# Small products, sums and a relu placed anew in a four-layer convolution kernel

## The chip, the core and the metric

The kernel runs on one core of one Trainium2 chip. A core has five engines that take instructions side by side: TensorE (PE in the profile; PEld is its loading of weights), VectorE (DVE), ScalarE (ACT), GpSimd (POOL) and SyncE (SP), which here issues transfers. Transfers (DMA) are issued by SP and by POOL. The metric is the device time of one launch in microseconds (us); lower is better.

## What is computed

The input x is 4 images of 256 channels with 56 x 56 positions, float32. Four layers follow one another, each of the form x = x + layer(gn(x)), where gn is a group normalization over 32 groups of 8 channels. Cut to what matters here:

```python
def _gn(v, G=32, eps=1e-5):
    g = v.reshape(B_, G, C_ // G, H_, W_)
    m = jnp.mean(g, axis=(2, 3, 4), keepdims=True)
    s = jnp.var(g, axis=(2, 3, 4), keepdims=True)
    return ((g - m) / jnp.sqrt(s + eps)).reshape(v.shape)
...
# layer 0: an involution. 7x7 kernels computed from h = 256 -> 64 channels at each
# position, one kernel for each group of 16 channels
out = (kern * patches).sum(axis=3)
# layer 1: relu(y + bn(conv3x3(relu(bn(conv3x3(y)))))) with y = gn(x)
# layer 2: an involution with batch norm and relu on h, and on its output
# layer 3: a spectral gate, x * (sigmoid factor of the channel) + x * (factor of the position)
```

The statistics of each normalization need the whole image of the layer before, so the layers meet at their norms: sums over an image, an average over the 8 channels of a group, a reciprocal root, and a scale ("rstd") and a shift for each channel.

## The kernel before

**Involution layers (0 and 2), `involution_layer`.** The work goes in 8 units (image b, half cb of the channels). A unit has two stages. In the *tap stage* (`tap_matrices`, L602) 32 pairs of PSUM banks are filled by products L613 of hp (the reduced channels) with the span weights z_sb, and read out into kt, two of three by DVE (L634), one of three by ACT (L627). In the *column stage* seven columns of 8 positions each are done by `apply` (L646): the products L659 of the windows xw with kt come in two parts, each into a pair of banks of its own; ACT (L672 in layer 0, L674 in layer 2) and DVE (L679, three in part 1 and one in part 2) read them into un, and POOL (L684, layer 0) or DVE (L686, layer 2) adds un to x in place. After each `apply` the next windows are made: seven transposes L427 on PE into a pair of banks, a copy by ACT (L439) and four transfers by SP (L445, L446); then `next_strip` writes the next normalized strip (POOL L412; in layer 2 from the third on, ACT L410). Layer 2 first clears the strip (L391, POOL), and DVE clears its borders (L404, L406).

PSUM is handed out by `two_banks` and `one_bank` from one pool of four pairs that are taken in turn; whoever takes a pair waits for the last reader of what it held.

**The order of the work.** Each engine executes its instructions in program order. Work of other kinds is put between the stages by hand: `tap_matrices` takes a dictionary `hooks` of steps to be issued at the tap position n (n - 0.5 before its read-out), and the columns have lists `early[tx]` and `late[tx]`, issued before and after column tx. Generators are cut into such steps by their yields. `by_counts(g, counts)` (L247) joins several yields of g to one step, as many as each count says.

**Norms, `norm_steps` (L217).** It yields after each of: the aggregation of sums (L215, DVE), a product with the group averages (L226, PE), the copy of its result (L229), a difference (L233), its square (L235), the sum with the variance (L237, all DVE), a second product (L240, PE), the reciprocal root (`rsqrt_eps`: L150 on DVE, L151 on POOL), and the shift (L244, DVE). It is given a function that says in which bank the two products go. In the involution layers, `norm_of` (L988) gives it `spare[0]`: in the column stages this is the second bank of the pair that the last part of `apply` took (set at L652), in the tap stages the end of the bank in use. The norms of layer 0's next image are made in the column stages of the image before: for cb = 0 in columns 3 to 6 (`norm_first`), for cb = 1 in columns 1 to 3 (`norm_last`), followed there by the channel reduction of that image. The last image's first unit has the steps for layer 1's norm of the images before, and layer 2's first unit those of its own last image.

**Channel reduction, `bottleneck` (L451).** Four products L467 of the shift with the reduction weights, their result with bias and scale as hb (L478 in layer 2, DVE), then the products L489 of x, whose results ACT writes as hp (L508 in layer 2, 20 of them an image) and DVE copies to the other half (L497).

**The convolutions (layer 1), `conv_layer`.** They run in 12 chunks of rows, three an image (16, 20 and 20 rows). In `conv2` the product L1606 or L1591 of each of six filter positions is combined by DVE (L1618 to L1634 and L1807 to L1813), partly after a copy by ACT (L1617). `joined(co)` ends a chunk for half co of the channels. For all chunks but the last two the residual comes in by accumulating transfers (`leaves`), and the chunk's sums are made by ACT with `mean_of` (L1768) and `spread_of` (L1774), each of which writes over x and so follows the store of it. Chunk 10: DVE adds y (L1752), ACT makes the relu (L1764), POOL issues a transfer that adds the layer's input (L1765), SP stores (L1766), and the sums are made by DVE's bn_stats (L1784) at the start of chunk 11, in pieces of up to 8 rows. Chunk 11, the last: DVE adds y (L1752), DVE makes the relu and adds the input in one instruction (L1757), SP stores (L1758); its six bn_stats stand in layer 2, all at hook 3 of the first tap stage. `tail` is the list of steps that a chunk leaves for later.

The boundary of layer 1 and layer 2 is then: the last chunk on PE and DVE, the norm of image 0 (whose parts are ready before, L244 excepted), L467, hb, L489, L508, two strips and two sets of windows, and the first L613.

## Time and profile before

| | us |
|---|---|
| three runs | 1665.92, 1666.82, 1667.41 |
| their median | 1666.82 |
| profiled execution | 1665.74 |
| its span, first to last instruction | 1663.7 |
| around the span | 2.0 |
| PE busy | 1586.3 |
| DVE busy | 1328.1 |
| ACT busy | 1010.6 |
| POOL busy | 552.1 |
| a column of layer 0 without a norm product | 4.13 |
| a tap stage | 22.5 |

The mean clock granted to PE was 0.979 of the full one. How to read the lines that follow: a timeline line has the start and the busy time in us, the engine, the line of the kernel, the operation, output<-inputs by the program's names, the shape, how many instructions were merged, and in brackets how long the engine had been idle before and which engine, tile and line ended that idle time. A line of the waits has the engine and the line that waited, what it waited for, the total in us, how many times, and the longest. The page's line of engines gives busy us, the share of the span and the number of instructions; the line below it in the prediction gives the shares of the chain that ended last.

### The profile page before, as it was taken

Reading aid. Unit: us, or ns where it says so; the run is one execution under the profiler, and the core shown is the slowest. Engines: PE = TensorE matmul, PEld = TensorE weight load, DVE = VectorE, ACT = ScalarE, POOL = GpSimd, SP = SyncE. Lnnn points to the kernel's source line nnn. Section 1 sums busy time; section 2 is a strip of 40 time slices with the busy share of each in tenths; the row PEclk is TensorE's granted clock in tenths of the full one; section 3 lists DMA queues with packets and bytes.
Section 4 is the critical chain, followed back from the end, with each engine's and each line's share of the span. In section 5 each row is a group of like instructions: output and inputs, shape, how many; then the busy total and the mean of one; then the engine's idle time right before and its main releaser. Section 6 shows DMA issues by size and latency. Waiting matters only on the chain.

```text
span 1663.7 us, 57362 instructions
## 1 busy us (share of the span) xinstructions
PE 1586.3 (95%) x24600; PEld 1442.0 (87%) x24600; DVE 1328.1 (80%) x2391; ACT 1010.6 (61%) x2203; POOL 552.1 (33%) x764
## 2 busy tenths in 40 slices
PE   6999999999989999999999999988999899899998
PEld 4997998898888898899999999976888888788886
DVE  2686887787659988899999999987777678678775
ACT  1655655557446565666666567426677577577565
POOL 2133223322522343423333333200000662662671
PEclk9999999999999999999999999998999999999997
DMA  2363445444558977987788797744445765764753
GB/s 92 111 197 115 157 155 169 146 156 132 181 171 266 171 130 150 198 174 157 159 166 170 163 197 151 172 144 145 131 140 166 216 220 188 210 216 159 206 168 113
DMA packets 102875, 275.67 MB, mean 166 GB/s; under 512 B 15877, under 2 KB 43790, under 8 KB 98910
## 3 DMA queue, kind: packets, MB, share of 16 engines
q0 software_dynamic: 43856, 106.25, 31.3%
q1 hardware_dynamic: 57726, 164.48, 30.7%
q8 instruction: 195, 3.19, 0.8%
q10 hardware_dynamic: 1040, 1.26, 0.3%
q14 instruction: 58, 0.48, 0.1%
HBM read 95.07 MB, written 49.15 MB: 87 GB/s over the span
## 4 chain that ended last, share of the span: by engine, by line
PE 68%; DVE 13%; DMA 6%; issue 6%; ACT 4%; SPq 1%; POOL 1%; ACTq 0%; POOLq 0%; DVEq 0%
PE ps L613 21%; PE mm L1606 17%; PE ps L659 15%; PE mm L1591 6%; DVE un L679 3%; PE ps L427 3%; DMA xw<-xw 2%; DVE kt L634 2%; PE ps L489 2%; DMA xs<-x 1%; ACT hp L508 1%; DMA xs<-v 1%; SPq L445 1%; DVE st L380 1%; ACT xs L1737 1%
## 5 line engine op out<-in xcount | busy, mean ns | idle before, releaser
L659 PE MATMUL ps<-kt,xw 126*32 126x48 f32 (+1 forms) x12544 | 378.9, 235 | 23.1 <-DMA xw<-xw 9.6
L659 PEld LDWEIGHTS ps<-kt,xw 126*32 126x32 f32 (+1 forms) x12544 | 340.9, 121 | 66.3 <-issue 40.4
L613 PE MATMUL ps<-hp,z_sb 64*126 64x133 f32 x6144 | 376.0, 278 | 1.8 <-ACT hp L508 0.9
L613 PEld LDWEIGHTS ps<-hp,z_sb 64*126 64x126 f32 x6144 | 364.1, 186 | 13.1 <-DVE kt L634 6.0
L634 DVE TENSOR_TENSOR kt<-ps,zb_sb 126x798 f32<-126x798 f32 x352 | 331.9, 980 | 48.9 <-PE ps L613 29.8
L627 ACT ACTIVATE kt<-ps,zb_sb 126x133 f32<-126x133 f32 x960 | 280.5, 441 | 78.1 <-PE ps L613 78.1
L1606 PE MATMUL mm<-xs,u_sb 128*128 128x140 f32 (+2 forms) x1664 | 210.3, 279 | 4.2 <-DMA xs<-v 4.1
L1606 PEld LDWEIGHTS mm<-xs,u_sb 128*128 128x128 f32 x1664 | 200.8, 192 | 4.6 <-issue 4.5
L1591 PE MATMUL mm<-v,u_sb 128*128 128x280 f32 (+2 forms) x864 | 193.9, 383 | 2.4 <-DVE hp L1622 1.7
L1591 PEld LDWEIGHTS mm<-v,u_sb 128*128 128x128 f32 x864 | 161.6, 189 | 28.0 <-PE mm L1606 2.2
L684 POOL TENSOR_TENSOR xs<-un,xs 128x240 f32<-128x240 f32 x112 | 72.0, 663 | 298.8 <-DVE un L679 298.7
L679 DVE SCALAR_TENSOR_TENSOR un<-ps,s,un 128x240 f32<-128x240 f32 x224 | 102.5, 458 | 85.2 <-ACT un L674 79.2
L679 DVE SCALAR_TENSOR_TENSOR un<-ps,par_sb,un 128x240 f32<-128x240 f32 x224 | 97.7, 456 | 84.3 <-ACT un L672 80.2
L1574 POOL DMA_DIRECT2D xs<-v x100 | 96.6, 1003 | 182.8 <-ACT xs L1573 161.7
L672 ACT ACTIVATE un<-ps,par_sb 128x240 f32<-128x240 f32 x112 | 50.2, 448 | 131.8 <-PE ps L659 121.0
L439 ACT COPY xw<-ps 126x896 f32<-126x896 f32 x112 | 101.3, 905 | 39.8 <-PE ps L427 22.0
L427 PE MATMUL ps<-ident_sb,strip_sb 128*126 128x128 f32 x784 | 112.7, 285 | 5.2 <-POOL strip_sb L412 2.0
L674 ACT ACTIVATE un<-ps,bn_t,s 128x240 f32<-128x240 f32 x112 | 60.1, 538 | 92.3 <-PE ps L659 85.2
L427 PEld LDWEIGHTS ps<-ident_sb,strip_sb 128*126 128x126 f32 x784 | 85.8, 142 | 16.1 <-POOL strip_sb L412 3.7
L1606 PE MATMUL mm<-v_sb,u_sb 128*128 128x140 f32 (+2 forms) x688 | 95.2, 281 | 3.2 <-ACT u_sb L1353 1.8
L1606 PEld LDWEIGHTS mm<-v_sb,u_sb 128*128 128x128 f32 x688 | 88.4, 193 | 4.3 <-ACT u_sb L1353 2.0
L1573 ACT ACTIVATE xs<-v 128x560 f32<-128x560 f32 (+2 forms) x100 | 61.8, 629 | 44.3 <-DVE v L1518 35.9
(325 smaller groups left out, 2344.2 us busy)
## 6 DMA issues: line engine op xcount, KB each, us to landing
xw<-xw SPq DMA_DIRECT2D x224, 252.0 KB
xw<-xw SPq DMA_DIRECT2D x224, 126.0 KB
xs<-x POOLq DMA_DIRECT2D x24, 560.0 KB, 6.9
x<-xs POOLq DMA_DIRECT2D x8, 1568.0 KB, 8.1
xs<-x SPq DMA_DIRECT2D x8, 1568.0 KB
xs<-v POOLq DMA_DIRECT2D x44, 280.0 KB, 4.3
xs<-v POOLq DMA_DIRECT2D x42, 252.0 KB, 4.2
xs<-in_x_dram SPq DMA_DIRECT2D x6, 1568.0 KB
```

What stands on the lines that cost most here:

```text
L427: nc.tensor.transpose(ps[:Q, k * P : (k + 1) * P], flat[:, k * Q : (k + 1) * Q], ident_sb)
L439: nc.scalar.copy(xw[:, :NSB, :], ps[:Q, : NSB * P].rearrange("q (n c) -> q n c", n=NSB))
L613: nc.tensor.matmul(ps[:Q, i, k * NT : (k + 1) * NT], z_sb[i * R : (i + 1) * R, cb * GB // 2 + gp, z0 : z0 + Q], hp[i * R : (i + 1) * R, py ...
L627: nc.scalar.activation(kt[:, g0 + i, pb, :, k], ps[:Q, i, k * NT : (k + 1) * NT], AF.Identity, bias=zb_sb[:, cb * GB + g0 + i, p0 + k : p0 ...
L634: nc.vector.tensor_tensor(kt[:, g0 : g0 + 2, pb], ps[:Q, :, : PB * NT].rearrange("q i (k t) -> q i t k", k=PB), zb_sb[:, cb * GB + g0 : cb ...
L659: nc.tensor.matmul(v[m * j : m * j + m, i, :, k * TP : (k + 1) * TP], xw[:, window(ty), m * j : m * j + m], kt[:, ng * j : ng * j + ng, :, ...
L679: nc.vector.scalar_tensor_tensor(part, o[e], s, part, ALU.mult, ALU.add)
L684: nc.gpsimd.tensor_tensor(dst, u, dst, ALU.add)
L1573: nc.scalar.mul(t[:, at], v[:, below], -1.0)
L1574: nc.gpsimd.dma_start(t[:, at], v[:, at], accum_op=ALU.add)
L1591: nc.tensor.matmul(ps, *position(u, v, ci, dy, k, co, n), start=(j == 0), stop=(j == NB * 3 - 1))
L1606: nc.tensor.matmul(ps[:, bank, co * m : (co + 1) * m], u[ci][:, co * P : (co + 1) * P], v2[:, : n // 2, ci * WT : (ci + 1) * WT], start=(c ...
```

## The change

Five things are changed.

1. `apply` no longer sets `spare`. The norm products of the column stages take a pair of their own from the pool (`one_bank`), by the new `norm_between`, which joins the steps as (1, 1, 4, 1, 1, 1): aggregation; product; the four DVE operations; product; root; shift. For cb = 0 of layer 0 they stand in columns 3, 4, 5, 6, 6, and the shift at hook 5 of the next unit's tap stage; for cb = 1 in the columns of before; in the two other places one step in each of the columns 1 to 6.
2. hb of layer 2 is made by ACT in place of DVE.
3. The sums of chunk 10 are made by ACT (`mean_of`, `spread_of`) behind position 5 of chunk 11, in place of DVE's bn_stats ahead of it.
4. In chunk 11, half co = 0 gets ACT's relu and POOL's accumulating transfer in place of DVE's one instruction; co = 1 stays. Both stores are issued by SP in layer 2, at hooks 3 and 5 of its first tap stage, and the six bn_stats stand singly at hooks 7 to 17.
5. The tile of the sums has room for both forms.

In program order this puts, on ACT: the sums, hb, the relu, then L508; on POOL: two memsets of the sums and the accumulating transfer ahead of the strip's memset L391; on SP: the two stores behind the first eight window transfers of layer 2.

```diff
@@ -475,7 +475,7 @@
                 if layer == 0:
                     nc.vector.tensor_add(hb, ps[:, 0:1], by_row(L0_RB))
                 else:
-                    nc.vector.scalar_tensor_tensor(hb, ps[:, 0:1], bn["s3"], bn["t3"], ALU.mult, ALU.add)
+                    nc.scalar.activation(hb, ps[:, 0:1], AF.Identity, bias=bn["t3"], scale=bn["s3"])
                 yield
                 weights = [redn[:, ci].rearrange("p i r -> p (i r)") for ci in range(NB)]
                 copies = []
@@ -649,7 +649,6 @@
                 y0 = 0
                 for ng, tys, nty, rows in O_PARTS:
                     pair = two_banks()
-                    spare[0] = pair[:, 1, :]
                     nb, m = len(tys), ng * GC
                     v = pair[:, :nb, : ng * nty * TP].rearrange("p i (e n) -> p i e n", e=ng)
                     for i in range(nb):
@@ -988,6 +987,9 @@
             def norm_of(layer, sts, u0, u1):
                 return norm_steps(sts, lambda: spare[0], layer, u0, u1)
 
+            def norm_between(layer, sts, u0, u1):
+                return by_counts(norm_steps(sts, one_bank, layer, u0, u1), (1, 1, 4, 1, 1, 1))
+
             hooks0 = {}
             if layer == 0:
                 place(hooks0, begin(), (1, 2, 4, 6, 7))
@@ -997,11 +999,12 @@
                 nc.sync.dma_start(zb_sb, zb2_dram)
                 next_strip()
                 run(bottleneck(0))
-                hooks0[3] = list(pending[0])
                 for _ in range(NXW - 1):
                     next_windows()
                     next_strip()
                 hooks0[7] = [next_windows, next_strip]
+                for n, f in enumerate(pending[0]):
+                    hooks0.setdefault(3 + 2 * n, []).append(f)
             if layer == 0:
                 next_strip()
                 for i in range(NXW):
@@ -1069,6 +1072,9 @@
                     n = 16 if layer == 0 else (26, 21)[cb]
                     hooks.setdefault(n, []).append(load_step(b + 1, cb))
 
+                if layer == 0 and cb == 1 and b + 1 < B:
+                    place(hooks, first, (5,))
+
                 last_image = layer == 0 and b == B - 1
                 if last_image and cb == 0:
                     g2 = tables2()
@@ -1090,21 +1096,21 @@
                                 late[j // 2].append(step(g))
 
                             def norm_first():
-                                yield from norm_of(0, {u + 2: sums_of[b + 1, 0]}, u + 2, u + 3)
-
-                            g = norm_first()
-                            for tx in (3, 4, 4, 4, 4, 4, 5, 5, 6):
+                                yield from norm_between(0, {u + 2: sums_of[b + 1, 0]}, u + 2, u + 3)
+
+                            g = first = norm_first()
+                            for tx in (3, 4, 5, 6, 6):
                                 late[tx].append(step(g))
                         else:
                             late[0] += [step(g)] * 4
                             late[1] += [step(g)] * 4
 
                             def norm_last():
-                                yield from norm_of(0, {u + 2: sums_of[b + 1, 1]}, u + 2, u + 3)
+                                yield from norm_between(0, {u + 2: sums_of[b + 1, 1]}, u + 2, u + 3)
 
                             g = norm_last()
                             late[1].append(step(g))
-                            late[2] += [step(g)] * 5
+                            late[2] += [step(g)] * 2
                             late[3] += [step(g)] * 3
                             g = bottleneck(b + 1)
                             late[3].append(step(g))
@@ -1122,12 +1128,12 @@
                     for tx in (1, 2, 4, 5) if cb == 0 else (0, 2, 3, 5):
                         late[tx] += [next_load, next_gate]
                 if last_image and cb == 0:
-                    g = norm_of(1, {}, 0, u)
-                    for tx in (1, 2, 2, 2, 2, 2, 3, 3, 4):
+                    g = norm_between(1, {}, 0, u)
+                    for tx in range(1, 7):
                         late[tx].append(step(g))
                 if layer == 2 and u == 0:
-                    g = norm_of(2, dict(enumerate(pending[1], NB * (B - 1))), NB * (B - 1), NB * B)
-                    for tx in (1, 2, 2, 2, 2, 2, 3, 3, 4):
+                    g = norm_between(2, dict(enumerate(pending[1], NB * (B - 1))), NB * (B - 1), NB * B)
+                    for tx in range(1, 7):
                         late[tx].append(step(g))
                 if last_image and cb == 0:
                     for tx in range(6):
@@ -1753,9 +1759,9 @@
                     x = xr_of[i, co][:, : n * W]
                     xj = x.rearrange("p (q j) -> p j q", j=4)
                     at = slice(y0 * W, y1 * W)
-                    if i == n_chunks - 1:
+                    if i == n_chunks - 1 and co == 1:
                         stt(xj, rj, 0.0, xj, ALU.max, ALU.add)
-                        nc.sync.dma_start(xout[bb][co][:, at], x)
+                        tail.append([lambda: nc.sync.dma_start(xout[bb][co][:, at], x)])
                     else:
                         added(x, xj, rj, co, at)
 
@@ -1763,7 +1769,11 @@
 
                     nc.scalar.activation(xj, rj, AF.Relu)
                     nc.gpsimd.dma_start(x, xin[bb][co][:, at], accum_op=ALU.add)
-                    nc.sync.dma_start(xout[bb][co][:, at], x)
+                    store = lambda: nc.sync.dma_start(xout[bb][co][:, at], x)
+                    if i < n_chunks - 1:
+                        store()
+                    else:
+                        tail.append([store])
 
                 def mean_of(st, x):
 
@@ -1780,8 +1790,9 @@
                 def stats(co, k):
 
                     r0, r1 = k * ST_ROWS, min(n, (k + 1) * ST_ROWS)
-                    at = sum(ST_PIECES[: i % 3]) + k
-                    nc.vector.bn_stats(sums[co][:, at, :], xr_of[i, co][:, r0 * W : r1 * W])
+                    at = 2 * k + (2 * ST_PIECES[0] + 1) * (i == n_chunks - 1)
+                    st = sums[co][:, at : at + 2, :].rearrange("p a b -> p (a b)")
+                    nc.vector.bn_stats(st, xr_of[i, co][:, r0 * W : r1 * W])
 
                 for n_s, k in enumerate(KS[:5]):
                     if n_s > 2:
@@ -1827,7 +1838,10 @@
                         joined(co)
                         run_all(after[10 + co])
 
-                if not summed or bb == B - 1:
+                if i == n_chunks - 2:
+                    for f in (mean_of, spread_of):
+                        tail.append([lambda co=co, f=f: f(sums[co][:, 2 * ST_PIECES[0]], xr_of[i, co][:, : n * W]) for co in range(NB)])
+                elif bb == B - 1:
                     tail += [[lambda co=co, k=k: stats(co, k) for k in range(ST_PIECES[i % 3])] for co in range(NB)]
 
 
@@ -1941,7 +1955,7 @@
                         sums_of[i // 3] = [
                             work.tile([P, 3, 3], F32, name="st3", bufs=4)
                             if i // 3 < B - 1
-                            else small.tile([P, sum(ST_PIECES), 6], F32, name=f"st_c{co}", bufs=1)
+                            else small.tile([P, 2 * (ST_PIECES[0] + ST_PIECES[2]) + 1, 3], F32, name=f"st_c{co}", bufs=1)
                             for co in range(NB)
                         ]
                     for k, f in enumerate(tail1):
@@ -1950,10 +1964,9 @@
                     if late_v is not None:
                         place(after, late_v, (0,) if i < n_chunks - 1 else ())
                         late_v = None
-                    loads_at = (2, 4) if i < n_chunks - 1 else (4, 7)
-                    for at, fs in zip(loads_at, tail2):
+                    for at, fs in zip((2, 4), tail2):
                         for k, f in enumerate(fs):
-                            after[at - (k == 0)].append(f)
+                            after[at - (k == 0) if i < n_chunks - 1 else 10].append(f)
                     tail2 = []
                     if i == 1:
                         last = [summed_columns(u2_sb, 3, ux2_sb[0], 4), summed_columns(u2_sb, 5, ux2_5, 3)]
```

## The prediction

> **What bounds the kernel now.** I read the page's busy shares first, then the chain of work that ended last, then the list of what TensorE (PE) waited for, then the timelines of the two stretches that the change touches.
>
> ```profile
> PE 1586.3 (95%) x24600; PEld 1442.0 (87%) x24600; DVE 1328.1 (80%) x2391; ACT 1010.6 (61%) x2203; POOL 552.1 (33%) x764
> PE 68%; DVE 13%; DMA 6%; issue 6%; ACT 4%; SPq 1%; POOL 1%; ACTq 0%; POOLq 0%; DVEq 0%
> ```
>
> PE is busy 95% of a span of 1663.7 us, so a change that leaves PE's products as they are (it does: the instruction counts of PE are equal in both programs) can win only from PE's gaps and from its half-clock stretches. PE's gaps over 0.2 us sum to 69.4 us, 10.7 of them at the start. The waits name them:
>
> ```profile
> PE ps L467 <- DVE hp L1624: 5.2, 1, 5.2
> PE ps L226 <- DVE un L679: 4.9, 7, 1.0
> PE ps L240 <- DVE un L679: 4.4, 8, 1.0
> ```
>
> (Total, times, longest.) The last two are the small norm products of the column stages, 9.3 us together: 7.4 in layer 0, two of 0.96 in layer 2. The first stands at the end of the convolutions.
>
> **Part 1: norm products in a pair of their own.** One column of layer 0, with its product:
>
> ```profile
> 139.66 0.98 PE L427 MATMUL ps<-ident_sb,strip_sb 128*126 128x128 f32 x7
> 139.70 1.75 DVE L679 SCALAR_TENSOR_TENSOR un<-ps,par_sb,un 128x240 f32<-128x240 f32 x4
> 141.50 0.38 PE L226 MATMUL ps<-mv_sb,gavg_sb 128*128 128x1 f32 x2 [0.85 <-DVE un L679]
> 141.81 3.29 PE L659 MATMUL ps<-kt,xw 126*64 126x96 f32 x112
> 146.52 0.38 PE L240 MATMUL ps<-d,gavg_sb 128*128 128x1 f32 x2 [0.50 <-DVE un L679]
> ```
>
> The window transposes end at 140.65; the product, which writes into the second bank of the column's part-2 pair, stands until the fourth L679 has read that pair at 141.45. In a pair of its own it waits for nothing still running: mv_sb was ready at 139.78. Removed: 7.4 + 1.9 = 9.3 us. The product itself (0.31) stays.
>
> What is late next: four pairs turn, and while one is held, part 1 of the next two columns gets the pair that the previous column's part 1 used, so it waits for that part's three L679. Here those end at 139.70 + 3 x 0.45 = 141.05, and part 1 comes at 140.65 + 0.31 = 140.96: a wait of 0.1. In the following column L679 begins at 144.65, its third ends at about 146.0, the windows end at 146.02: nothing. Only the first product of the three units with cb=1, where other DVE work stands before L679, costs about 0.15 each (0.45), and three units in which a pair is taken again for the channel reduction (L489) about 0.3 each (0.9). In layer 2 I book 0.2. The bounds: nothing, and, where an additional pair is in use today,
>
> ```profile
> 1359.66 3.23 PE L659 MATMUL ps<-kt,xw 126*64 126x96 f32 x112 [0.54 <-DVE un L679]
> ```
>
> 0.42 to 0.78 (three such waits) for each of two columns at 16 products. I take the layer-0 estimate, since it is read from the very columns. Part 1: -7.4 + 1.35 - 1.9 + 0.2 = **-7.7**. The DVE steps of the norms move by a column at most; they are 0.14 to 0.6 us each, and their reader, the next unit's preparation, is columns away. The shift that goes to the next unit's tap stage (0.16 us on DVE) is cheap there.
>
> **Part 2: the end of the last chunk.** The chain as it is:
>
> ```profile
> 1109.92 0.63 DVE L1784 BATCH_NORM_STATS2 st_c<-u_sb 128x6 f32<-128x448 f32 x1 [3.43 <-DMA u_sb<-x]
> 1111.52 1.19 PE L1606 MATMUL mm<-v_sb,u_sb 128*128 128x140 f32 x8 [1.34 <-DVE hp L1622]
> 1124.54 1.01 PE L467 MATMUL ps<-norm_sb,red_sb 128*128 128x1 f32 x4 [5.16 <-DVE hp L1624]
> 1125.94 2.20 DVE L1757 SCALAR_TENSOR_TENSOR xs<-u_sb,xs 128x1120 f32<-128x1120 f32 x1
> ```
> ```profile
> 1131.62 0.17 DVE L244 SCALAR_TENSOR_TENSOR norm_sb<-gm,norm_sb 128x2 f32<-128x2 f32 x1
> 1133.29 8.34 ACT L508 ACTIVATE hp<-ps,hb,bn_s 64x168 f32<-64x168 f32 x20 [22.27 <-DVE hb L478]
> 1135.92 1.73 PE L427 MATMUL ps<-ident_sb,strip_sb 128*126 128x128 f32 x7 [1.99 <-ACT hp L508]
> 1138.86 1.75 PE L427 MATMUL ps<-ident_sb,strip_sb 128*126 128x128 f32 x7 [1.22 <-POOL strip_sb L412]
> 1141.47 7.82 PE L613 MATMUL ps<-hp,z_sb 64*126 64x133 f32 x96 [0.85 <-ACT hp L508]
> 1147.43 2.78 DVE L1784 BATCH_NORM_STATS2 st_c<-xs 128x6 f32<-128x448 f32 x6
> ```
>
> DVE first waits 3.43 us for an accumulating transfer, does 3.07 us of sums (0.63 + 0.91 + 0.62 + 0.91), and is then busy without a gap to 1131.79, while ACT idles 22.27 us. The 20 activations L508, 8.34 us, run behind that and end just after the first L613, the start of layer 2's taps.
>
> Removed from DVE: wait and sums, 6.5 us. Not all of it comes through: the next DVE step then waits for ACT's copy at 1108.30 (ends 1108.70), the one behind for PE, which without its 1.34 us stall ends its last convolution product at 1118.0 in place of 1119.4. Walking the same DVE durations from there, L1624 ends at 1119.75 in place of 1124.49: -4.7. Then one L1757 (2.20) leaves DVE, and L244 ends at about 1125.1 in place of 1131.8.
>
> What takes its place on ACT: of chunk 10, two sums of 1.124 + 0.190 us (the row of L1771), four small operations of 0.20 and two squares of 1.229 + 0.187 (L1778): 6.3 us from 1113.8, when the stores of that chunk have landed (1113.69 and 1115.10, and the sums write in place), to about 1120.3. hb moves to ACT behind L467 at 1121.1 (0.2 us). The relu (rows of L1764: 2.28 us) needs L1752 of co=0, which ends at 1121.2; margin 0.9 us. So relu 1121.2 to 1123.5, L508 from there to 1131.85. Before: to 1141.63. ACT's side is -9.8. PE's side: L489 is at half clock from 1120.7 to about 1127.6, POOL's memset and strip (0.83 + 0.89) start at L244's 1125.1, first windows 1128.2, second strip 1131.1, second windows 1132.9, first L613 at 1133.0: -8.4. The middle of the two is -9.1; PE's side is the one that ends last, so I lean to it: **-8.9**.
>
> Queues: POOL gets two memsets and the accumulating transfer's issue (0.88) ahead of its strip memset; it waits for the relu at 1123.5, done by 1124.4, before the 1125.0 at which the memset could go. SP: both stores go behind the first eight window transfers of layer 2; the four loads behind them now wait for L1757 of co=1 (1124.9) and the relu; z_sb, which took 3.9 us from issue to landing, is there at about 1130.2, ahead of 1133.0. The accumulating transfer lands 5.2 to 11.2 us after its issue (20 earlier ones, median 7.5): 1129 to 1135.6, its sums come at the seventh tap position, about 1138.6; so no wait.
>
> The six sums at 1147.43 now stand singly at six positions: the two PE gaps they make (0.40 and 0.48) and part of the stage's excess go. DVE needs 22 x 0.943 + 2.78 = 23.5 us there against 22.5 of PE; the excess today is 3.5 with the half clock, then 1 to 2.5: **-1.0**. hb on ACT in the three other images: PE waits for another engine, 0 to 0.2 us each; nothing booked.
>
> The clock row: TensorE ran at half from 1121.76 to 1128.59, which follows the 5.16 us gap, and again from 1135.41 to 1145.65, though no gap there is over 1.99 us. The Trainium skill, "TensorE: Matmul & The Clock Gate", section "Why this matters for your kernels", asks for no idle gaps over about 3 us to keep the clock. This trace contradicts it: gaps of 1.99 and 1.22 within 5 us were followed by 10.2 us at half. By that rule the changed boundary, whose longest gap I work out as 1.8 us, would have no half clock at all, and the sum would be an estimated 3 to 5 us lower.
>
> **Sum.** -7.7 - 8.9 - 1.0 = -17.6. The profiled execution took 1665.74 us: 1648.1. The runs' median (1666.82) lies 1.1 above it: **1649**.
>
> **Rivals.**
> *Only the bank pairs pay.* At the boundary another releaser takes the place: ACT's sums overrun (margin 0.9 us), the z_sb load or the accumulating transfer lands late (4 us of margin and 3 by the median). For it: four new waits in one stretch of 20 us; against: each has its margin. All of part 2 gone: -7.7, 1659.
> *Only the boundary pays.* The three pairs that turn make part 1 wait as long as the product did: 16 x 0.58. For it: the 0.54 row above; against: the third L679's end at 141.05 against 140.96. -9.9: 1657.
> *The clock comes back too.* With no gap over 2 us the half-clock stretches at the boundary (17 us of them) shrink. They cost PE 1.4 us at L489 (24 products in 6.81; at full clock 16 take 3.60), 1.5 in two L427 (1.73 and 1.75 for 0.98) and 2.2 in the first 96 L613 (7.82; 384 take 22.5 at full clock), of which I count 4.4: -22, 1645. Against it: the second stretch came after short gaps.
> *Slower.* While a pair is held, two part 1s per product wait for L679. At 0.78 each, 32 x 0.78 = 25.0; less 9.3 and 9.9 that is +5.8: 1672. It decides from the point at which the third L679 ends over 0.4 us behind the windows' end in most such columns; in the columns read it is -0.05 to 0.4.
> *The change does nothing*: the scheduler puts the products where the same L679 holds them and the boundary is set by ACT either way: 1666 to 1668.
>
> **How the numbers follow.** Forecast (1645.5 to 1653, both parts at their bounds) 0.58; only the pairs 0.12; only the boundary 0.12; the clock too 0.10; slower 0.05; nothing 0.03. The range runs from 1643.5 to 1659.5; it leaves out the slow and the null case and a little at each end. 0.2% (3.3 us) is about what a measurement of this kernel can tell: faster 0.92, same 0.03, slower 0.05.
>
> **What would show it.** In the changed profile the waits of L226 and L240 for L679 are gone, and those of L659 for L679 grow by less than 3 us; L1624 to L467 is a gap near 1.8; ACT's last L508 ends 16 to 18 us before the same point of today's span; the first L613 follows a wait for ACT or POOL under 1 us. I am wrong if L659 waits for L679 at most products, if the relu starts late behind ACT's squares, if L613 waits for a DMA, or if DVE's sums wait for the accumulating transfer.

## The result and the profile after

The changed kernel took 1645.32 us (median of 4 runs, 1640.02 to 1653.34) for 1666.37 of the kernel before (4 runs, 1664.09 to 1667.41): a ratio of 0.988, 95% interval 0.9835 to 0.9924. Measured once more beside more runs of before (6 runs, 1648.68; before 1665.02 in 29 runs) the ratio was 0.9898, interval 0.9874 to 0.9923. By these ratios that is 20 and 17 us less. 1649 had been forecast. The profiled execution of the changed kernel took 1647.77 us.

Its page, the span and the line of engines:

```profile
span 1645.4 us, 57403 instructions
PE 1578.3 (96%) x24600; PEld 1437.5 (87%) x24600; DVE 1325.7 (81%) x2380; ACT 1020.9 (62%) x2220; POOL 556.0 (34%) x767
```

PE has as many products as before and 8 us less busy time, because its clock is granted more often: mean 0.985 for 0.979, 52 us in all at half clock for 73, and 14 of these 21 us lie around the boundary. The other 10 us of the 18.3 us by which the span is shorter came out of its gaps. What PE waits for now (in the changed kernel the lines from L652 on are one lower, those of the convolutions named here six higher):

```profile
PE ps L658 <- issue: 12.9, 19, 1.7
PE ps L292 <- ACT xs L284: 10.9, 1, 10.9
PE ps L658 <- DMA xw<-xw: 7.7, 13, 1.3
PE ps L658 <- DVE un L678: 6.6, 16, 1.2
...
PE ps L467 <- DVE hp L1630: 2.0, 1, 2.0
PE ps L613 <- ACT xw L439: 1.8, 1, 1.8
```

The waits of the norm products (9.3 us) are gone from the list, and L467 waits 2.0 in place of 5.2. The waits of L658 (the old L659) for L678 (the old L679) have grown from 2.5 to 6.6 us, and the "issue" of L658, idle time that nothing in the profile ends, is 12.9 where it was 9.0. The same column as in the prediction, from the timeline:

```profile
139.42 0.98 PE L427 MATMUL ps<-ident_sb,strip_sb 128*126 128x128 f32 x7
139.46 1.75 DVE L678 SCALAR_TENSOR_TENSOR un<-ps,par_sb,un 128x240 f32<-128x240 f32 x4
140.24 0.28 PE L226 MATMUL ps<-mv_sb,gavg_sb 128*128 128x1 f32 x2
141.01 3.53 PE L658 MATMUL ps<-kt,xw 126*64 126x96 f32 x112 [0.48 <-DVE un L678]
144.47 0.98 PE L427 MATMUL ps<-ident_sb,strip_sb 128*126 128x128 f32 x7
145.29 0.28 PE L240 MATMUL ps<-d,gavg_sb 128*128 128x1 f32 x2
```

The product has no bracket any more: it runs in the shadow of the transposes. What was 0.85 us ahead of it is now 0.48 ahead of the next column's part 1. From one set of transposes to the next this column takes 5.05 us (144.47 - 139.42) where it took 5.37.

The end of the convolutions:

```profile
1110.20 1.14 ACT L1781 ACTIVATE u_sb<-u_sb 128x1120 f32<-128x1120 f32 x1 [2.21 <-DMA x<-u_sb]
...
1115.89 1.23 ACT L1788 ACTIVATE u_sb<-u_sb,c 128x1120 f32<-128x1120 f32 x1
...
1116.76 0.61 PE L467 MATMUL ps<-norm_sb,red_sb 128*128 128x1 f32 x4 [2.02 <-DVE hp L1630]
1117.02 0.19 ACT L1788 ACTIVATION_READ_ACCUMULATOR u_sb<-u_sb,c 128x1 f32 x1
...
1118.16 2.26 ACT L1770 ACTIVATE xs<-u_sb 128x1120 f32<-128x1120 f32 x1 [0.40 <-DVE u_sb L1758]
...
1120.35 8.37 ACT L508 ACTIVATE hp<-ps,hb,bn_s 64x168 f32<-64x168 f32 x20
1120.71 0.91 POOL L1771 DMA_DIRECT2D xs<-x  x1 [16.67 <-ACT xs L1770]
...
1121.56 0.15 DVE L244 SCALAR_TENSOR_TENSOR norm_sb<-gm,norm_sb 128x2 f32<-128x2 f32 x1
...
1122.72 1.03 SPq L998 DMA_DIRECT2D z_sb<-z_dram  x1
...
1129.65 5.81 PE L613 MATMUL ps<-hp,z_sb 64*126 64x133 f32 x96 [1.78 <-ACT xw L439]
```

ACT's sums end at 1117.21 and its relu begins when DVE delivers, at 1118.16: 0.95 us of room, 0.35 of it used by hb. From the last convolution product (1114.74) to the first L613 it takes 14.9 us where it took 22.1. And 96 of L613 take 5.81 us in place of 7.82: the clock is full there. Stretches of this profile show it (window, length, then busy time and instructions of PE, PEld, DVE, ACT and POOL, then the granted clock, the DMA share, GB/s):

```profile
1117.00:1121.00 4.00, 4.00 (x16) 1.47 (x17) 3.97 (x3) 3.41 (x6) 0.29 (x1) 0.63 0.00 0
1121.00:1125.00 4.00, 4.00 (x23) 1.64 (x20) 2.81 (x6) 3.92 (x11) 2.60 (x7) 0.95 0.72 104
1129.00:1133.00 4.00, 3.35 (x58) 3.38 (x60) 2.18 (x3) 3.25 (x7) 0.00 (x0) 1.00 0.36 114
```

### The profile page after: what moved, and what is told of

Read it like the earlier page. It is cut to its first block, busy times and chain, and to the rows that moved or that the text cites. A ratio compares the mean times of both kernels' runs of the same rounds, so it can differ in the third digit from the quotient of the medians.

```text
span 1645.4 us, 57403 instructions
## 1 busy us (share of the span) xinstructions
PE 1578.3 (96%) x24600; PEld 1437.5 (87%) x24600; DVE 1325.7 (81%) x2380; ACT 1020.9 (62%) x2220; POOL 556.0 (34%) x767
## 4 chain that ended last, share of the span: by engine, by line
PE 75%; DVE 10%; DMA 4%; ACT 4%; issue 4%; POOL 1%; SPq 1%; ACTq 0%; POOLq 0%; DVEq 0%
PE ps L613 21%; PE mm L1612 20%; PE ps L658 16%; PE mm L1597 8%; PE ps L427 3%; DVE un L678 3%; DVE kt L634 2%; DMA xw<-xw 2%; PE ps L489 2%; ACT hp L508 1%; DMA xs<-v 1%; DVE st L380 1%; DMA xs<-x 1%; PE ps L971 1%; PE ps L741 1%
## 5 line engine op out<-in xcount | busy, mean ns | idle before, releaser
L658 PE MATMUL ps<-kt,xw 126*32 126x48 f32 (+1 forms) x12544 | 379.2, 234 | 29.7 <-issue 12.9
L658 PEld LDWEIGHTS ps<-kt,xw 126*32 126x32 f32 (+1 forms) x12544 | 340.2, 121 | 75.5 <-issue 49.3
L613 PE MATMUL ps<-hp,z_sb 64*126 64x133 f32 x6144 | 373.3, 277 | 3.1 <-ACT xw L439 1.8
L613 PEld LDWEIGHTS ps<-hp,z_sb 64*126 64x126 f32 x6144 | 361.6, 185 | 13.4 <-DVE kt L634 5.3
L678 DVE SCALAR_TENSOR_TENSOR un<-ps,s,un 128x240 f32<-128x240 f32 x224 | 102.5, 458 | 79.9 <-ACT un L673 75.8
L678 DVE SCALAR_TENSOR_TENSOR un<-ps,par_sb,un 128x240 f32<-128x240 f32 x224 | 98.3, 456 | 80.7 <-ACT un L671 76.6
L439 ACT COPY xw<-ps 126x896 f32<-126x896 f32 x112 | 101.4, 906 | 39.5 <-PE ps L427 21.9
```

The costliest lines, as they stand in the source:

```text
L439: nc.scalar.copy(xw[:, :NSB, :], ps[:Q, : NSB * P].rearrange("q (n c) -> q n c", n=NSB))
L613: nc.tensor.matmul(ps[:Q, i, k * NT : (k + 1) * NT], z_sb[i * R : (i + 1) * R, cb * GB // 2 + gp, z0 : z0 + Q], hp[i * R : (i + 1) * R, py ...
L658: nc.tensor.matmul(v[m * j : m * j + m, i, :, k * TP : (k + 1) * TP], xw[:, window(ty), m * j : m * j + m], kt[:, ng * j : ng * j + ng, :, ...
L678: nc.vector.scalar_tensor_tensor(part, o[e], s, part, ALU.mult, ALU.add)
```

## The experiments

**What was to be told apart.** By the profile of the changed kernel the boundary had paid what was forecast, the column stages of layer 0 little of the 6.0: the seven with a product are together 1.5 us shorter by the trace (the expectations below say 0.9). Theory A: what the products no longer wait for comes back as stalls of PE for its own instructions, since the new "issue" gaps end soon after packets of the instruction queue land; it would also explain the spread of the times. Rival B: the pairs pay in full, and one execution showed it badly. Theory C puts the spread on the end of the chunk.

All times are compared with runs of the kernel before on the same chip: 1665.02 us (29 runs, 1657.68 to 1673.28) for the first four, 1665.01 (13 runs) for the next four, 1661.41 (15 runs) for the last three. "Boundary" is the time from the last convolution product to the first L613, "taps" that stage up to the first column of layer 2.

**The changed kernel once more**, unchanged.

> The changed kernel once more, for its spread. Four runs of it lay between 1640.0 and 1653.3 us, four of the kernel before between 1664.1 and 1667.4. Theory A: the column stages are now at the pace at which PE's instructions arrive (PE stands for nothing that the profile shows, 25 times, 16 us in all, each time 0.9 to 1.9 us after a 16 KB packet of the instruction queue has landed; in the kernel before 10 times, 10 us), and how long such a packet waits behind the window transfers differs from run to run. Then the times spread over 8 us or more again, with a median near 1645, and the sum of these stalls goes up and down with the time. Rival B: the spread was a chance of four runs; then 1643 to 1648, with a spread like that of before, 3 to 4 us.

1648.68 us (6 runs, 1645.78 to 1652.62), ratio 0.9898 (0.9874 to 0.9923). The spread is no property of the changed kernel: with 29 runs the kernel before spreads over 15.6 us. So theory A falls in this point. Its other half needed experiments of its own; the gaps of L658 that end 1.1 to 1.75 us behind an instruction packet summed to 10.2 us here (14 of them) after 14.6 (23).

**Only the norm products' pairs**, on the kernel before, with the column lists of the change and nothing of it at the end of layer 1.

```diff
-                    spare[0] = pair[:, 1, :]
+            def norm_between(layer, sts, u0, u1):
+                return by_counts(norm_steps(sts, one_bank, layer, u0, u1), (1, 1, 4, 1, 1, 1))
...
```

> Only the norm products' pairs of their own, on the kernel before. The prediction gave this part -7.7 us, 1658 to 1659. In the changed kernel's profile the waits of L226 and L240 for L679 (9.3 us) are gone, but the column stages of layer 0 are only 0.9 us shorter in all, and the one of layer 2 1.5. Theory A (part of it comes back as stalls for instructions): 1661 to 1665, with a spread above 5 us. Rival B (the full part 1, and the profiled execution had bad luck with its transfers): 1657 to 1660.

1657.83 us (12 runs), ratio 0.9954 (0.9932 to 0.9976): -7.7 us by the ratio, interval -4.0 to -11.3 (the medians lie 7.2 apart). Rival B holds: the part is worth about what had been worked out. The profiled execution of the changed kernel had shown little of it in layer 0 because other waits fell into the same stages. Where none did, a column stage of layer 0 takes 29.5 and 36.1 us (units with cb = 0 and 1) with pairs of their own, 30.4 and 36.95 with the products in their old place. Its waits:

```profile
PE ps L658 <- issue: 7.3, 9, 1.5
PE ps L658 <- DVE un L678: 6.2, 16, 1.2
PE ps L467 <- DVE hp L1629: 5.2, 1, 5.2
```

The new wait for L678 comes with this part (6.2 us), L467's old 5.2 stays, and the "issue" is no higher than before the change (7.3 for 9.0 us, one execution of each). From one execution to another it differs by more: 5.6 to 13.8 us over the eleven profiles with 112 products a column. So nothing shows that this part makes it.

**Only the end of the last chunk**: the changed kernel with the norm products, and the columns of their steps, as before.

```diff
+                    spare[0] = pair[:, 1, :]
-                return by_counts(norm_steps(sts, one_bank, layer, u0, u1), (1, 1, 4, 1, 1, 1))
...
```

> Only the end of the last chunk (sums and relu on ACT, the accumulating transfer, the late stores, hb on ACT), with the norm products where they were. The prediction gave it -9.9. From the two profiles: conv end to first tap product 14.9 us for 22.1, the 1.34 us gap before it gone, the tap stage 2.3 shorter, together -10.8. Theory A: 1655 to 1657, with the stalls for instructions and the spread as before the change (3 to 4 us). If the end of the chunk were also what spreads the times (theory C: the late stores and the accumulating transfer land at random), the spread would be 8 us here and 3 in the run with the pairs alone.

1657.66 us (12 runs, 1652.57 to 1664.30), ratio 0.9959 (0.9938 to 0.9980): -6.8 us, -3.3 to -10.3; the -9.9 of the forecast lies at the edge of that, the -10.8 expected here outside. Theory C falls: the 12 runs spread over 11.7 us here and over 16.1 with the pairs alone. The boundary took 14.67 us, as in the changed kernel, but the taps 27.42 where that has 25.55. Clock and waits of this execution say why its taps are longer:

```profile
1118.00:1122.00 4.00, 2.90 (x19) 1.41 (x13) 2.59 (x6) 3.92 (x11) 2.89 (x8) 1.00 0.67 99
1122.00:1126.00 4.00, 1.45 (x7) 1.05 (x7) 1.54 (x3) 3.92 (x10) 0.78 (x1) 0.65 0.83 268
1126.00:1130.00 4.00, 3.89 (x34) 3.92 (x36) 1.82 (x2) 2.12 (x3) 0.00 (x0) 0.50 0.36 114
```
```profile
PE ps L226 <- DVE un L679: 4.3, 7, 1.0
PE ps L240 <- DVE un L679: 3.9, 7, 1.0
...
PE ps L613 <- DMA z_sb<-z_dram: 1.8, 1, 1.8
```

The first block is stretches again. Here 6.8 us at half clock, from 11.8 us behind the last convolution product on, fell on the first L613; in the changed kernel it was one stretch of 3.4 us, 3.3 us behind that product, on L489, where it costs little. The same instructions got the one or the other in different executions: of the nine profiles with this end of the chunk, six had the short stretch and three the long. And the first L613 waits for a transfer, of which below.

**The norm products in the free columns of the windows' pair.**

```diff
                 begun_windows.append(ps)
+                beside[0] = ps[:, NSB * P :]
-                return by_counts(norm_steps(sts, one_bank, layer, u0, u1), (1, 1, 4, 1, 1, 1))
+                return by_counts(norm_steps(sts, lambda: beside[0], layer, u0, u1), (1, 5, 1, 1, 1))
...
```

> The changed kernel, but the norm products of the column stages go into the 128 free columns of the pair that the seven window transposes fill, and the four DVE steps stand in the product's own column again. No pair is taken more, so part 1 of the next column waits for L678 as little as in the kernel before: the 6.6 us of such waits (16 times) fall to about 2.5 (5 times, layer 2). If these waits are a real loss: 4 us faster, 1641. Theory A: in layer 0 half of it or more turns into stalls for instructions, 1642 to 1645. Slower than 1647 only if the product waits for ACT's copy L439 of the same pair (0.9 us x 16).

1663.70 us (12 runs), ratio 0.9982 (0.9958 to 1.0006): of the changed kernel's 17 us 3 are left (at most 7), less than the 6.8 of the end alone, though these two intervals overlap. The gain of the pairs is gone. It is the last sentence of the expectation that happened:

```profile
PE ps L240 <- ACT xw L440: 8.3, 8, 1.0
PE ps L226 <- ACT xw L440: 8.3, 8, 1.0
```

16 products, each 1.04 us late: they write other columns of the pair than ACT's copy (L440 here) reads, and they wait for the copy all the same: in this program a product waits by the bank or by the pair (no run tells these two apart), not by the columns. Which bank a small product goes into decides whose reading it waits for.

**Without the second half of the window transfers**.

```diff
-                return (0, NSB, 2 * NSB - 1)[j] + k
+                return (0, NSB, NSB)[j] + k
-                for j in range(1, TY):
+                for j in range(1, TY - 1):
```

> The changed kernel without the second half of the window transfers: the windows shifted by two rows are left out, and the products that need them take those shifted by one row, so the outputs of two involutions are not the reference's. PE has the same products; SP has two transfers a column in place of four, and the DMA engines carry some 250 KB less a column. Theory A (instruction packets wait behind window transfers): the stalls that end 0.9 to 1.9 us after an instruction packet fall from 16 us to under 4, the waits for xw and the other short gaps of L658 go too, and the time falls by 12 to 25 us, to 1620 to 1633, with a small spread. If the instructions come at a pace that no other transfer changes (A2), the stalls stay at 12 to 16 us and only the xw waits (7.7) go: 1637 to 1640.

1638.85 us (4 runs), ratio 0.9858 (0.9816 to 0.9900; by the interval 1634 to 1648 us, so A's 1620 to 1633 lie outside). It is the number of A2, by which other transfers don't change the pace of the instructions:

```profile
PE ps L658 <- issue: 13.6, 21, 1.5
PE ps L292 <- ACT xs L284: 10.8, 1, 10.8
PE ps L658 <- DVE un L678: 5.3, 13, 1.2
```

The waits for xw are gone from the list; the "issue" gaps are where they were, 13.6 us. Halving the number of the window transfers did not lessen them, so theory A's "behind the window transfers" falls too.

**A column's second part in wide products**, which stream 96 columns of kt in place of 48.

```diff
+                            wide = ng == 2 and k < nty - 1
+                            if wide and k % 2:
+                                continue
...
```

> The changed kernel with the nine products of a column's second part made as four of twice the width and one: 80 of PE's 112 products a column are left, 64 of some 240 instructions fewer, with the same columns streamed (the moving data are other ones, so the outputs of both involutions are not the reference's). The transfers are the same. Theory A: with 27% fewer instructions to be fetched a column the stalls behind instruction packets are gone (under 2 us), beside the same xw waits; the time falls by 12 to 20 us if a wide product takes as long as two. If PE stands for the windows and not for instructions (rival B), the gaps of L658 stay within 4 us of the 27.8 that they are. A wide product may stream slower or faster than two narrow ones: the column's own busy time in the profile tells that apart from the gaps.

1633.37 us (4 runs), ratio 0.9807 (0.9773 to 0.9841), by the ratios 15 us below the changed kernel, where 12 to 20 were expected. Counted by time alone, 9 gaps with 6.7 us end 1.1 to 1.75 us behind an instruction packet (14 and 23 of them, 10.2 and 14.6 us, in the changed kernel's two profiles), not under 2. But each of the 9 has another releaser in the profile (ACT's copy 4, window transfers 3, DVE 2); the "issue" gaps of these products, 9.8 and 12.9 us in the changed kernel, are gone from the list, as theory A expected. L658 was busy 358.2 us for 379.7. But the other gaps of the column stages rose:

```profile
PE ps L665 <- DMA xw<-xw: 14.9, 13, 2.6
PE ps L665 <- DVE un L685: 11.2, 24, 1.3
...
PE ps L665 <- ACT xw L439: 4.4, 6, 0.9
```

A layer-0 column stage took 29.1 to 30.0 and 36.05 us, hardly less than the 29.5 and 36.1 with 0.2 us more of products a column (21.5 us over 112 columns): behind PE the next pace, DVE's L685 (the old L679) and ACT's copy, stands already close. On the packets this run alone is suggestive only, since it changed PE's busy time as well.

**Chunk 10's sums by DVE again, the rest as changed.**

```diff
-                if i == n_chunks - 2:
-                    for f in (mean_of, spread_of):
...
+                    loads_at = (2, 4) if i < n_chunks - 1 else (4, 7)
...
```

> The changed kernel, but chunk 10's sums are made by DVE's bn_stats again (six in chunk 11), with the last chunk's relu on ACT and its transfer and stores as changed. Expected from the first profile: the 3.43 us wait and the 1.34 us gap come back, L467 stands 4.5 to 5.2 us, the chain ahead of the relu starts 4.7 us later: 5 us slower than the changed kernel, about 1650. If ACT's sums were on the path (the rival that they delay the relu), it would be less than 2 us slower.

1650.38 us (10 runs, 1641.16 to 1659.24), ratio 0.9908 (0.9881 to 0.9936): 1.7 us above the changed kernel by the ratios where 5 were expected, and the intervals overlap: by the time alone no difference can be told. In the trace it is plain: L467 waits 5.2 us again,

```profile
PE ps L467 <- DVE hp L1630: 5.2, 1, 5.2
PE mm L1612 <- DVE hp L1628: 2.4, 1, 2.4
```

and the boundary takes 18.30 us for 14.4 to 14.9, the taps 25.76 as in the changed kernel. The sums on ACT are worth 3.4 to 3.9 us there and the gap ahead of it.

**Only the sums on ACT;** relu, sum and stores of the last chunk as before, and the six bn_stats at hook 3 again.

```diff
-                    if i == n_chunks - 1 and co == 1:
+                    if i == n_chunks - 1:
                         stt(xj, rj, 0.0, xj, ALU.max, ALU.add)
+                        nc.sync.dma_start(xout[bb][co][:, at], x)
...
```

> The changed kernel, but the last chunk's relu, sum and store are DVE's and SP's as before, and the six bn_stats stand at hook 3 again; only chunk 10's sums stay on ACT (and hb). Expected: the chain L1758, L1763, L1758, L1763 on DVE keeps L244 2.2 us later, L508 starts behind hb as early as 1117.8 rather than 1120.35 since no relu is ahead of it, and the first tap product follows the strip memset: 1 to 3 us slower than the changed kernel at the boundary, and 1 to 2 in the tap stage through the bn_stats, 1647 to 1650. If ACT's relu ahead of L508 is what bounds the changed boundary, it is no slower at the boundary than the changed kernel.

1643.25 us (4 runs, 1643.11 to 1648.26), ratio 0.9883 (0.9851 to 0.9914): faster than expected and not to be told from the changed kernel. In the trace, boundary 15.65 and taps 28.03: 3.2 to 3.5 us more than the changed kernel's 14.4 to 14.9 and 25.6 to 25.8 together, most of it in the taps, where 6.8 us at half clock and the six bn_stats in a row fell. So the relu on ACT gains only some 1 us ahead of the first L613. ACT pays 2.3 us for it ahead of L508; what it saves, DVE's 2.2 us ahead of L244, brings POOL's strips earlier (PE waits 2.7 us for strips at the boundary here, 1.2 in the changed kernel).

**The norm products in part 1's second bank**, with the changed end.

```diff
+                    if ng == GB // 2:
+                        spare[0] = pair[:, 1, :]
...
```

> The changed end of the last chunk, and the norm products neither in a pair of their own nor in the bank of the column's second part, but in the second bank of its first part's pair, with the steps in the columns of before. The product then waits for the third L679 of its column in place of the fourth: in the timeline that the prediction showed, 141.05 in place of 141.45, windows' end 140.65, so 0.4 for 0.85 and about 0.05 for 0.50; layer 2 about 0.5 for 0.96. Sum of the products' waits 2.5 to 3.5 us (9.3 before), and part 1 waits for L679 as before (2 to 2.5, against 6.2 to 6.9 with pairs of their own). If only such waits count, it is level with the changed kernel, 1644 to 1649, and 6 to 8 us faster than the end of the chunk alone. If the pairs of their own gain by something else, it stays at the 1657 of the end alone.

1648.26 us (10 runs, 1641.21 to 1655.16), ratio 0.9919 (0.9892 to 0.9946), as expected level with the changed kernel. Its waits:

```profile
PE ps L226 <- DVE un L680: 2.7, 7, 0.6
...
PE ps L240 <- DVE un L680: 1.7, 7, 0.3
PE ps L660 <- DVE un L680: 1.4, 4, 0.4
```

5.8 us in all, 6.6 in the changed kernel, 11.8 in the kernel before. The products' own waits are 4.4 of it, where 2.5 to 3.5 were expected. By these waits what counts is that the product no longer waits for the fourth reading; a pair of its own is one way to that. By undisturbed column stages (29.9 and 36.4 us in layer 0) pairs of their own are still 0.3 to 0.4 us a unit better.

**The run just shown (part 1's second bank), with the load of z_sb ahead of two small loads.**

```diff
-                nc.sync.dma_start(sin_sb, cs[:, H:])
-                nc.sync.dma_start(cs2_sb, cs2)
                 nc.sync.dma_start(zb_sb, zb2_dram)
+                nc.sync.dma_start(sin_sb, cs[:, H:])
+                nc.sync.dma_start(cs2_sb, cs2)
```

> The run before, and layer 2's load of z_sb and zb_sb is issued ahead of the two small loads on SP. In the changed kernel z_sb took 5.1 to 6.5 us from issue to its last packet, beside the accumulating transfer, for 3.7 to 3.9 without it, and the first L613 came 6.5 to 7.2 us after the issue, with the last L508 at 6.0 to 6.6. The issue moves up by about 0.8 us. If z_sb bounds the first L613, conv end to first L613 falls from 14.4 to 14.9 us to about 13.8; if ACT's L508 does, it falls by less than 0.3. In the time, 1643 to 1649, not to be told from the run before.

1646.83 us (6 runs), ratio 0.9906 (0.9873 to 0.9938). Boundary 14.43 us for 14.94 in the run just shown, 0.5 less, between the two that were expected. What ended the idle time of the first L613, there and here:

```profile
PE ps L613 <- DMA z_sb<-z_dram: 1.9, 1, 1.9
```
```profile
PE ps L613 <- DVE hp L497: 1.3, 1, 1.3
```

Here it starts 7.30 us behind the issue, right after DVE's copy L497 (which ends at 7.20) of what ACT's L508 wrote, and the load's packets have ended at 6.12: now ACT's chain bounds it and no longer the load. The changed kernel's second profile had 14.44 without this edit, so it is worth at most half a microsecond.

**Part 1's products in halves**, same result.

```diff
-                                    v[m * j : m * j + m, i, :, k * TP : (k + 1) * TP],
...
+                                for e in range(0, ng, 2):
...
+                                        v[m * j : m * j + m, i, e : e + 2, k * TP : (k + 1) * TP],
...
```

> The changed kernel with each of the 20 products of a column's first part made as two of half the width, by the same weights loaded twice: 152 products a column in the profile for 112, some 320 instructions of PE for 240, same result, same transfers, same columns streamed. If the stalls behind the packets of the instruction queue are PE standing for its instructions (a packet holds 256), the pace of the packets (4.7 to 5.3 us apart where PE stands) makes a column last about 320/256 x 5 = 6.2 us in place of 4.1, mostly as gaps that end 1.1 to 1.75 us behind a packet: 30 to 110 us slower. If the packets have nothing to do with it, the time grows only by the weights loaded twice (40 x 0.03 = 1.1 us a column at most, 60 us), as busy time, and the number of such gaps stays at 14 to 25.

1741.56 us (2 runs), ratio 1.0476 (1.0415 to 1.0536). Both of the expectation's costs came: PE's busy time rose by 58 us (1636.0 for 1578.3), and the gaps did this:

```profile
PE 1636.0 (94%) x29080; PEld 1501.9 (87%) x29080; DVE 1325.3 (76%) x2380; ACT 1020.0 (59%) x2220; POOL 553.6 (32%) x767
```
```profile
PE ps L659 <- issue: 51.3, 68, 2.7
...
PE ps L427 <- issue: 7.5, 8, 2.6
```

Of L659's gaps, 70 with 52.6 us end 1.1 to 1.75 us behind the landing of a 16 KB packet of the instruction queue (the changed kernel: 23 with 14.6 and 14 with 10.2), and only 1.8 us are of other kinds; the waits for xw vanish. All but two of them stand at multiples of 125 to 128 products from one another, and a product is two instructions in the trace: some 256, a packet. The queue carried 230 such packets for 195. This part of theory A is shown: PE stands for its instructions where it uses them faster than they come. What sets the pace at which they come no run here shows.

## Why the prediction was right, step by step

- **The sum, -17.6**: measured -20 and -17. The first median, 1645.32, lies 0.2 below the band of 1645.5 to 1653 that the forecast gave its main case, the second, 1648.68, within it. The two parts, each alone, gave -7.7 (interval -4.0 to -11.3; forecast -7.7) and -6.8 (-3.3 to -10.3; forecast -9.9). Together 14.5, and both at once -17.0 (-12.8 to -21.0): within the intervals the parts simply add. That the first part meets its forecast to the tenth is chance, with an interval of that width.
- **Products' waits removed, 9.3**: gone to the last one. The trace of before had read them rightly: the product waited for a bank, not for its data.
- **What is late next**: the mechanism, part 1 waiting for L678 of the column before, was right, its size too small: over the whole kernel it grew by 4.1 us where under 3 was forecast. In layer 0 the new waits are 2.1 to 2.3 us at part 1 and 0.3 to 0.6 at L489 (forecast 0.45 and 0.9), in layer 2's first unit 0.5 (forecast 0.2). I had placed the end of the product 0.31 us behind the transposes, so that part 1 came late by itself; it runs with them, part 1 is ready sooner and waits 0.48 where 0.1 was forecast. The stage came out as forecast even so, because the product's own time, which the forecast left in, went into that wait. The two errors offset each other, and that is luck. Where nothing else falls into them, the stages are 0.9 us (cb = 0, four units) and 0.85 (cb = 1, three units) shorter with pairs of their own, 6.2 us in all (forecast 6.0), and layer 2's first unit 1.5 (forecast 1.7). Averaged with their disturbances, over five profiles with pairs and two without, the seven stages differ by 4.7.
- A sign that I had named for being wrong, "L659 waits for L679 at most products", came true without the forecast failing: a wait that comes in place of a longer one is still a gain. The test should have been the column's length, not a count. Another 3.5 to 4.0 us of the same wait stand in the rest of layer 2, where the change moves no product, in three profiles with pairs of their own (1.4 to 2.5 in three without). Why is not settled.
- **ACT's last L508** was to end 16 to 18 us earlier than in the profile of before. It ended 12.9 us earlier in the first profile and 14.7 in the second. From the end of the convolutions on, ACT was near the forecast (-9.6 and -9.0 with the gap at L1606, forecast -9.8); most of what is missing is layer 0, which gave 1.5 and 3.0 us of the 6.0 in these two executions.
- **Boundary**: L467's gap forecast 1.8, measured 2.02. ACT's margin ahead of the relu forecast 0.9, measured 0.95. Gap at L1606 (1.34) gone, boundary -7.2 and -7.6: -8.5 to -9.0 for a forecast of -8.9.
- **The release of the first L613** was forecast wrongly, at ACT or POOL under 1 us. It was 1.78 and 1.3 us, and in the first profile the load ended it: the sign "L613 waits for a DMA", named for being wrong, came true. The line above names ACT's L439, whose end falls together with the semaphore of the load's landing, both 6.8 us behind the issue; but in the second profile L613 starts 0.95 us before L439 ends, so it doesn't wait for that. I had given the z_sb load the 3.9 us that it took before. Beside the accumulating transfer (packets from 0.4 us ahead of the load's issue to 3.8 behind it) its packets ended 6.3 us after the issue; in the profiles with that transfer 4.5 to 6.5, in the three without it 3.7 to 3.9. The margin of nearly 3 us was so used up, and load and L508 end within a microsecond of each other. It cost little only because L508 ends there too, which is luck as well.
- **Taps, -1.0**: measured -2.1 to -2.3 in the changed kernel, -0.4 where the half clock fell on them. So the clock had a share in the size, beside the bn_stats.
- **The rival "the clock comes back too"** (chance 0.10) is in part what happened: from 17.1 us at half clock around the boundary to 3.4 in both profiles of the changed kernel. Here the longest gap of PE is 2.02 us, and half clock still came, for 3.4 or for 6.8 us, by execution. The Trainium skill, "TensorE: Matmul & The Clock Gate", section "Why this matters for your kernels", asks for no idle gaps of PE over about 3 us between bursts of products, so that the clock doesn't fall. The measurement decides: in this kernel gaps under that bound were not enough to keep it.
- **The slower rival** did not come: it needed 0.78 us at most of the 32 places, and the waits at the products' places stayed at 0.5 or less, seven of them in layer 0. No wait of DVE for the accumulating transfer appeared.

## What to carry to other kernels

In this kernel a small product that shared a bank waited for that bank's last reader, even when it wrote columns that the reader did not touch (16 times 1.04 us); look at who reads a bank last, and give the product one whose readers are done. Judge such a move by the length of the stage, not by which waits appear in the list, since part of each wait only moves. And a load whose latency was measured alone need not keep it when the same change puts another transfer beside it: here 3.7 to 3.9 us became 4.5 to 6.5.

## What the hardware showed besides

Unexpected was what PE's instructions cost. In column stages, where PE goes through some 240 instructions in 4.1 us, it stands for them: PE then goes on 1.1 to 1.7 us behind a packet's landing, and where neighbouring packets both have such a gap they land 3.9 to 6.6 us apart in the changed kernel (median 5.0; with the halved products 3.5 to 7.2, median 4.4). By this count the kernels with 112 products a column lose 7 to 15 us to it, differently from one execution to the next, and 52.6 us go with some 320 instructions a column. The Trainium skill, "Runtime: NRT & Kernel Launch", section "Instruction fetch mechanics", says that instructions come in blocks of 16 KiB, fetched while the block before is executed, and that the cost of a block's border is mostly hidden. The size agrees with the packets here. Mostly hidden agrees with the kernels with 112 products a column, where 10 to 23 of the 195 packets show such a gap, on products that follow one another by 29 ns on average; with the halved products it is 70 of 230, and the cost is no longer small.
